# Transposing the later contexts on VectorE ahead of time, and shorter spreads, in a gated cross-attention kernel

## The chip, the cores and the metric

The kernel runs on one core of a Trainium2 chip. The metric is the device time of one launch in microseconds, a median over runs. Five engines take instructions in order, each from its own queue: TensorE (matmuls and transposes through an identity; PE in the profile, its weight loads PEld), VectorE (DVE), ScalarE (ACT), GpSimd (POOL) and SyncE (SP), which here issues nearly all DMAs. TensorE writes to PSUM, which has eight banks of 128 partitions by 512 floats; all else works in SBUF with 128 partitions. Semaphores let one engine wait for another.

## The reference

All data are float32. Four batches have 256 queries of width 512 and a context of 1601 rows of width 512. First comes cross-attention with 32 query heads of width 128 in 8 groups, each group with one key head and one value head; then a feed-forward step with eight low-rank experts.

```
q = (layernorm(x) @ Wq + bq).reshape(B, L, 8, 4, 128)
k, v = split(ctx @ Wkv + bkv)            # 8 heads of 128 each
attn = softmax(einsum('blkgd,bmkd->bkglm', q, k) / sqrt(128))
o = einsum('bkglm,bmkd->blkgd', attn, v)
x = x + tanh(g_xattn) * (o @ Wo + bo)
h = layernorm(x)
x = x + tanh(g_ffn) * (h @ base_W.T + 2 * sum over the top 2 of 8 experts)
```

## The kernel before

**Groups.** The main loop runs over 64 groups: batch b (4), key head h (8), half l of the queries (2). I number them 0 to 63 in that order, so batch 0 has groups 0 to 15. One group scores 128 queries of four heads (512 columns) against 1601 keys in 13 tiles, 12 of 128 rows and one of 65. `score_unit` (L1142) makes the scores for one or two tiles, ScalarE copies them out (L1151) and VectorE folds them into a running maximum (`fold`, L1067 to L1073). `softmax` spreads the maximum, subtracts it (L1181), takes the exponential (L1184), and folds a sum. `av_unit` (L1233) multiplies the group before with V: `run_group` alternates the scores of this group with the V products of the previous one. Then `window(now)` fills the time with other TensorE work, the tasks: key and value products of the next pair of heads (`pair_steps`, L896 and L907), query products, output products.

**Spread.** The maxima stand per partition and must go to all partitions (`spread`, L1076). VectorE joins two halves (L1106), transposes in 32x32 blocks (L1107), reduces each block (L1086) to 16 values per partition. Three copies bring the four groups of 32 partitions side by side (L1090), a second reduction joins them (L1093), three copies bring the result back to all four groups (L1097), and a transpose of the broadcast value spreads it (L1100). For the sums, the copies are made on GpSimd and the reciprocal stands between; for the maxima all is on VectorE.

**Block products.** The key, value and query products use Strassen's scheme with seven block products instead of eight. They need the context turned (features on partitions) and three sums of its four blocks, and one block replaced by a difference. A block is a half of the context rows by a half of the features. The turned context stands in `ctxT` (both halves of the rows, 801 columns each with the 65 rows left over split in two, and a column of zeros), the sums in `T`, the left-over rows in `rest`.

**Later contexts.** Batch 0's context is turned in the opening stretch. For batches 1 to 3 `ctx_steps` does it in one place: as soon as the last value pair of the batch before has used `ctxT` (group 12, 28 or 44), its 13 steps each load 128 context rows (L672), transpose four 128x128 blocks on TensorE into a bank (`turn_ctx`, L258), have ScalarE copy them to `ctxT` (L260), and after every second tile queue three subtractions on VectorE (`ctx_sums`, L723). `last_sums` (L734, L738) makes the last differences. After that the key products of the new batch's first pair can begin.

**Planner.** The order on each engine is written out by a planner that runs in Python while the program is built. It keeps a clock for TensorE (`now`), VectorE and ScalarE. `later` puts a piece of VectorE or ScalarE work with a cost and a ready time into one of ten queues (`sub`, `oT`, `so`, `exp`, `ln`, `T`, `norm`, `sum`, `low`, `low_a`). `pump` takes the piece that can start first, and of equals the one in the earlier queue. `force` takes a piece and all that it needs at once. A task has steps with a cost, a ready time and a due group. Weights are planned to be there 6000 ns after their load is issued (`LAG_PAIR`), context tiles 1700 ns (`LAG_CTX`). Buffers that exist once (`wq`, `wkv`, `wo`, `ctxT`, `T`) make a load wait on SP until the last reader is done. Weights and their sums are stored to DRAM when first made, in batch 0 for the most part, and loaded ready-made afterwards.

## Time and profile before

| what | value |
|---|---|
| median of 3 runs | 2557.84 us (2557.19 to 2559.42) |
| span of the profiled execution | 2555.5 us; the page gives no other time for it |
| TensorE busy | 2547.3 us |
| VectorE busy | 2202.6 us |
| ScalarE busy | 1188.1 us |
| GpSimd busy | 150.4 us |
| DMA | 167.16 MB, mean 65 GB/s |

Busy time is the union of an engine's instructions, without those that only wait or issue DMAs. Each float32 matmul appears as two records, each transpose as one. Matmuls are pipelined, so their records overlap: the cost of one is the distance to the next start, not its duration. The groups 13, 29 and 45, which hold the transposes of contexts 1 to 3, lie at 579.7 to 617.9, 1161.3 to 1192.5 and 1823.8 to 1861.2 us.

### The profile page before, as it was taken

The numbers are of one execution on the slowest core, as the hardware profiler recorded it, in microseconds if no ns is written. First come the engines' busy times: TensorE is split into PE (matmuls) and PEld (weight loads), VectorE is DVE, ScalarE is ACT, GpSimd is POOL, SyncE is SP. The second block draws the span as 40 slices with busy tenths as digits, with TensorE's granted clock in tenths as the row PEclk, the third lists the DMA queues.
The fourth block names the chain that finished last, engine by engine and source line by source line (L and its number), as shares of the span: only waits on it lengthen the run. The fifth ranks groups of instructions, "written<-read, shape, count | busy, mean of one in ns | idle before, by whom it ended". The sixth has DMA issues, their size and how long they took to land.

```text
span 2555.5 us, 26175 instructions
## 1 busy us (share of the span) xinstructions
PE 2547.3 (100%) x9235; PEld 1487.8 (58%) x9235; DVE 2202.6 (86%) x3310; ACT 1188.1 (46%) x1897; POOL 150.4 (6%) x401
## 2 busy tenths in 40 slices
PE   9999999999999999999999999999999999999999
PEld 7557566565555656455565665756656455555554
DVE  4889898899889989899788887878889899998897
ACT  3544454445434555455444444445454445544551
POOL 0000000000000000110000000000000000000000
PEclk9999999999999999999999999999999999999999
DMA  4313222324110111012121111212221011111000
GB/s 158 123 64 108 87 95 84 114 85 149 48 56 23 44 52 56 25 40 83 49 81 37 62 52 62 81 48 81 85 84 56 25 52 52 52 44 52 17 17 33
DMA packets 75499, 167.16 MB, mean 65 GB/s; under 512 B 5372, under 2 KB 32028, under 8 KB 72808
## 3 DMA queue, kind: packets, MB, share of 16 engines
q1 hardware_dynamic: 74424, 164.41, 19.3%
q8 instruction: 73, 1.20, 0.2%
q0 software_dynamic: 416, 0.81, 0.1%
q14 instruction: 58, 0.48, 0.1%
q10 hardware_dynamic: 528, 0.26, 0.0%
HBM read 119.06 MB, written 46.40 MB: 65 GB/s over the span
## 4 chain that ended last, share of the span: by engine, by line
PE 99%; DVE 1%; DMA 0%; ACT 0%; issue 0%; DVEq 0%; ACTq 0%
PE av L1233 28%; PE sc L1142 28%; PE pxk L896 6%; PE pxv L907 6%; PE pxq L896 4%; PE pyk L896 3%; PE pyv L907 3%; PE po L1310 3%; PE pox L484 3%; PE pyq L896 2%; PE pzk L896 2%; PE pzv L907 2%; PE poy L484 1%; PE pzq L896 1%; PE ptv L1020 1%; PE pk L803 1%
## 5 line engine op out<-in xcount | busy, mean ns | idle before, releaser
L1142 PE MATMUL sc<-qT,kT 128*128 128x512 f32 (+1 forms) x1664 | 775.9, 592 | 0.0
L1151 ACT COPY p<-sc 65x512 f32<-65x512 f32 x820 | 474.3, 586 | 636.5 <-PE sc L1142 575.2
L1233 PE MATMUL av<-p,v 65*128 65x512 f32 x1640 | 766.1, 592 | 1.2 <-ACT p L1184 1.2
L1233 PEld LDWEIGHTS av<-p,v 65*128 65x128 f32 x1640 | 309.5, 190 | 376.2 <-issue 370.8
L1142 PEld LDWEIGHTS sc<-qT,kT 128*128 128x128 f32 (+1 forms) x1664 | 307.0, 186 | 374.3 <-issue 340.4
L1181 DVE TENSOR_TENSOR p<-p,mb 65x512 f32<-65x512 f32 x442 | 485.9, 1137 | 0.1
L1184 ACT ACTIVATE p<-p 65x512 f32<-65x512 f32 x442 | 423.1, 990 | 38.6 <-DVE p L1181 34.5
L1073 DVE TENSOR_TENSOR mx<-mx,p 128x1024 f32<-128x1024 f32 x252 | 308.1, 1223 | 137.9 <-ACT p L1151 134.8
L1073 DVE TENSOR_TENSOR sm<-sm,p 128x1024 f32<-128x1024 f32 x252 | 307.4, 1220 | 9.8
L1090 POOL COPY quad_sm<-quad_sm 32x16 f32<-32x16 f32 x186 | 70.7, 380 | 2088.3 <-DVE quad_sm L1086 2083.1
L896 PE MATMUL pxq<-xq,wq 128*128 128x256 f32 x512 | 131.2, 379 | 0.0
L941 ACT ACTIVATE kT<-pxk,biasT 128x384 f32<-128x384 f32 (+1 forms) x120 | 57.9, 508 | 141.8 <-PE pxk L896 141.0
L896 PEld LDWEIGHTS pxq<-xq,wq 128*128 128x128 f32 x512 | 92.5, 189 | 31.2 <-issue 15.3
L941 ACT ACTIVATE qT<-pxq,biasT 128x256 f32<-128x256 f32 x64 | 30.3, 473 | 140.2 <-PE pxq L896 140.2
L944 ACT COPY v<-pxv 128x384 f32<-128x384 f32 x90 | 43.0, 477 | 104.8 <-PE pxv L907 104.8
L896 PE MATMUL pxk<-T,wk 128*128 128x417 f32 (+1 forms) x240 | 90.4, 499 | 0.0
L907 PE MATMUL pxv<-wv,T 128*128 128x128 f32 x720 | 90.2, 275 | 0.0
L896 PE MATMUL pxk<-ctxT,wk 128*128 128x417 f32 (+1 forms) x240 | 90.0, 499 | 0.0
L907 PE MATMUL pxv<-wv,ctxT 128*128 128x128 f32 x720 | 90.0, 275 | 0.0
L907 PEld LDWEIGHTS pxv<-wv,T 128*128 128x128 f32 x720 | 86.4, 192 | 4.7 <-issue 4.3
L907 PEld LDWEIGHTS pxv<-wv,ctxT 128*128 128x128 f32 x720 | 86.4, 192 | 4.7 <-issue 4.3
L1067 DVE TENSOR_TENSOR mx<-p,p 128x1024 f32<-128x1024 f32 x63 | 76.8, 1220 | 13.1 <-ACT p L1151 12.8
(264 smaller groups left out, 2809.6 us busy)
## 6 DMA issues: line engine op xcount, KB each, us to landing
wo<-in_L_xattn_Wo_dram SPq DMA_DIRECT2D x18, 1024.0 KB, 5.3
kept_q<-wq SPq DMA_DIRECT2D x16, 896.0 KB, 4.8
wq<-kept_q SPq DMA_DIRECT2D x16, 896.0 KB, 5.1
wo<-kept_wo SPq DMA_DIRECT2D x13, 1024.0 KB, 5.8
wk<-kept_k SPq DMA_DIRECT2D x11, 896.0 KB, 4.6
wv<-kept_v SPq DMA_DIRECT2D x11, 896.0 KB, 4.4
ctx<-in_ctx_dram SPq DMA_DIRECT2D x36, 256.0 KB, 2.7
wq<-in_L_xattn_Wq_dram SPq DMA_DIRECT2D x32, 256.0 KB, 3.1
```

The costliest lines, as they stand in the source:

```text
L484: nc.tensor.matmul(bk[:, :HD], left[i]()[:, c, :], blk[:, c, :], start=first and c == 0, stop=c == 1, skip_group_check=True,)
L896: nc.tensor.matmul(bk[:, :n], a(SLOT[i], c), operand(i, c, s, n), start=first and c == 0, stop=c == 1, skip_group_check=True,)
L907: nc.tensor.matmul(bk[:, t * HDIM : (t + 1) * HDIM], operand(i, c, s + t * P, P), a(SLOT[i], c), start=first and t == 0 and c == 0, stop=c ...
L941: nc.scalar.activation(dst, src, AF.Identity, bias=bias_of(kind, h0 + f))
L1067: nc.vector.tensor_tensor(acc, p[first], p[first + 1], op)
L1073: nc.vector.tensor_tensor(acc, acc, p[j], op)
L1142: nc.tensor.matmul(sc[:r, :], kT_t[b, h][:, key_col(i) : key_col(i) + r], qT_t[b, h][:, :, l * P : (l + 1) * P], start=True, stop=True,)
L1151: nc.scalar.copy(p[:r, k, :], sc[:r, :])
L1181: nc.vector.tensor_tensor(p, p, m, ALU.subtract)
L1184: nc.scalar.activation(p, p, AF.Exp, scale=scale)
L1233: nc.tensor.matmul(av, v_t[b, h][:r, i, :], p_t[key][j][:r, k, :], start=(j == 0 and k == 0), stop=(j == NPAIR - 1 and k == len(pairs[j]) ...
L1310: nc.tensor.matmul(po, oT_t[key][:, g, :], w_t["o", b, h][:, g, :], start=(g == 0), stop=(g == G - 1),)
```

## The change

**Later contexts.** `ctx_steps` no longer loads or transposes. A new function `swap_ctx(b, n)` handles one of 13 units of a context, early. A unit is 128 rows from each half of the context by half of the features (the 13th: 64 of the 65 left-over rows). Two SP loads bring the four pieces into one staging buffer of 128 by 512, VectorE transposes it in 32x32 blocks into a second buffer, three subtractions make four further planes, and eight stores (four for the 13th unit) write both buffers to a DRAM tensor `kept_ctx` of 2048 rows by 801 columns, in pieces of 32 floats. The DRAM addresses complete the transpose, since each block goes to its place. The very last context row goes a way of its own, with two small loads, three small subtractions and two small stores. The pieces go into a new, last queue `turn`.

Units of contexts 1 and 2 are called from group 0 on, one ahead of each group, a second one behind the scores of groups 1, 4, 7, 9 and 10, and none in groups 16, 17, 19, 21, 22 and 23; those of context 3 from group 32 on, one per group. A unit first forces the unit before it to be stored. `ctx_steps` then loads `ctxT`, `T` and `rest` with eleven SP loads from `kept_ctx`, when the last value pair of the batch before is done; `LAG_CTX` is 40000 ns. One subtraction on `rest` is left for VectorE. GpSimd clears the column of zeros for batch 0 only.

**Spread.** The three copies and the second reduction become two pairwise operations on VectorE, between the upper and lower 64 and then 32 partitions; the way back is two copies instead of three (32 to 64 partitions, then 64 to 128). For the sums only the way back is on GpSimd.

**x steps.** The layernorm steps and the first query weights of batch 2 become a task two groups earlier (ahead of group 21 instead of 23), due two groups earlier (28 instead of 30).

```diff
@@ -122,7 +122,7 @@
     clock = {"now": 0.0, "v": 0.0, "a": 0.0, "hold": 0.0}
     free = [0.0] * NBANK
     done = {}
-    queues = {q: deque() for q in ("sub", "oT", "so", "exp", "ln", "T", "norm", "sum", "low", "low_a")}
+    queues = {q: deque() for q in ("sub", "oT", "so", "exp", "ln", "T", "norm", "sum", "low", "low_a", "turn")}
 
     def vec(ns, ready=None):
 
@@ -151,7 +151,7 @@
         fn()
         clock[engine] = start + ns
         if key is not None:
-            done[key] = start + ns + SEM + (GP_COPIES if key[0] == "part" and key[2] < 4 else 0)
+            done[key] = start + ns + SEM + (GP_COPIES if key[0] == "part" and key[2] == 3 else 0)
 
     def pump(until=NEVER, most=None):
 
@@ -582,7 +582,7 @@
         xa_t[b] = pool.tile([P, NL, D], F32, tag=f"xa{b}", name=f"xa_{b}", bufs=1)
     STAGE = 2
 
-    LAG_DMA, LAG_CTX, LAG_X = 2500, 1700, 3000
+    LAG_DMA, LAG_CTX, LAG_X = 2500, 40000, 3000
 
 
     JOINT = 2
@@ -643,9 +643,6 @@
         return [(0, ready, begin)] + [f(*t) for t in tiles for f in (norm, turn)] + [(0, 0, sums)]
 
 
-    ctx_order = [i + k * (HK // P) for i in range(HK // P) for k in range(2)]
-    ctx_order += range(FULL, KT)
-
     def ctx_col(i):
 
         half, t = divmod(i, HK // P)
@@ -658,46 +655,113 @@
     def new_ctx(b):
         ctxT_t[b] = pool.tile([P, NC, 2 * HW], F32, tag="ctxT", name=f"ctxT_{b}", bufs=1)
         rest_t[b] = pool.tile([P, NC, REST], F32, tag="rest", name=f"rest_{b}", bufs=1)
-        if REST0 < HT:
+        if REST0 < HT and b == 0:
 
             nc.gpsimd.memset(ctxT_t[b][:, :, REST0:HT], 0.0)
 
+    ctx_kept = {}
+    NUNIT = HK // P * 2 + 1
+
+    def swap_ctx(b, n):
+
+        if n:
+            force(("kept", b, n - 1))
+        else:
+            ctx_kept[b] = dram.tile([8 * D // 2, HW], F32, tag=f"ctx_{b}", name=f"kept_ctx_{b}")
+        kept_b = ctx_kept[b].rearrange("(j k) w -> k j w", k=32)
+        m, q = divmod(n, 2)
+        src, dst = (
+            pool.tile([P, 4, P], F32, tag="stage", name=f"{kind}_{b}_{n}", bufs=STAGE)
+            for kind in ("ctx", "swap")
+        )
+        last_n = n == NUNIT - 1
+        r = 64 if last_n else P
+        for half in range(2):
+            if last_n:
+                assert REST == 65 and REST0 == 32
+                k0 = FULL * P + 32 * half
+                for c in range(2):
+                    nc.sync.dma_start(
+                        src[32 * c : 32 * c + 32, half::2, :],
+                        ctx_kv[b, k0 : k0 + 32, :].rearrange("k (s q c) -> k q s c", s=2, q=2)[:, c],
+                    )
+            else:
+                k0 = half * HK + m * P
+                nc.sync.dma_start(
+                    src[:, half::2, :],
+                    ctx_kv[b, k0 : k0 + P, :].rearrange("k (s q c) -> k q s c", s=2, q=2)[:, q],
+                )
+
+        flat = lambda t: t[:r].rearrange("k s c -> k (s c)")
+
+        def sums(S, R):
+            nc.vector.tensor_tensor(R[:, 0:2], S[:, 1::2], S[:, 0:2], ALU.subtract)
+            nc.vector.tensor_tensor(R[:, 2], S[:, 3], R[:, 0], ALU.subtract)
+            nc.vector.tensor_tensor(R[:, 3], S[:, 2], R[:, 2], ALU.subtract)
+
+        def swap():
+            nc.vector.transpose(flat(dst), flat(src))
+
+        def store():
+            for a in range(r // 32):
+                lo, q_ = (0, a) if last_n else (HT + m * P + 32 * a, q)
+                for i, t in enumerate((dst, src)):
+                    j = (2 * q_ + i) * 16
+                    nc.sync.dma_start(
+                        kept_b[:, j : j + 16, lo : lo + 32],
+                        t[32 * a : 32 * a + 32].rearrange("k s (j w) -> k (s j) w", w=32),
+                    )
+
+        later("turn", "v", 710, clock["now"] + LAG_DMA, swap)
+        later("turn", "v", 900, 0.0, lambda: sums(dst[:r], src[:r]), ("swap", b, n))
+        later("turn", "v", 0, ("swap", b, n), store, ("kept", b, n))
+        if last_n:
+            one = small.tile([P, 8, 2], F32, tag="one", name=f"one_{b}", bufs=1)
+            nc.gpsimd.memset(one, 0.0)
+            for i in range(2):
+                nc.sync.dma_start(
+                    one[:, 1 + 2 * i], ctx_kv[b, LK - 1, :].rearrange("(s q p) -> p s q", s=2, q=2)[:, i]
+                )
+
+            def end():
+                for q_ in range(2):
+                    nc.sync.dma_start(
+                        ctx_kept[b].rearrange("(q o p) w -> p q o w", q=2, o=8)[:, q_, :, HT - 1],
+                        one[:, :, q_],
+                    )
+
+            later("turn", "v", 500, clock["now"] + LAG_DMA, lambda: sums(one[:, :4], one[:, 4:]), ("swap", b, n + 1))
+            later("turn", "v", 0, ("swap", b, n + 1), end, ("kept", b, n + 1))
+
     def ctx_steps(b):
 
...
         def begin():
+            force(("kept", b, NUNIT))
             new_ctx(b)
             new_sums(b)
...
+            ct, rest, (T, tt) = ctxT_t[b], rest_t[b], T_t[b]
+            kept_b = ctx_kept[b].rearrange("(q o p) w -> p o q w", q=2, o=8)
+            for dst, o in (
+                (ct[:, 0:2, :HW], 0),
+                (ct[:, 2:4, :HW], 2),
+                (T[:, 1], 6),
+                (ct[:, 0:2, HW:], 5),
+                (T[:, 0], 4),
+                (T[:, 2], 7),
+                (ct[:, 2:4, HW:], 3),
+                (rest[:, 0:2, :REST0], 0),
+                (rest[:, 2:4, :REST0], 2),
+                (rest[:, 0:2, REST0:], 1),
+                (rest[:, 2:4, REST0:], 3),
+            ):
+                nc.sync.dma_start(dst, kept_b[:, o, :, : dst.shape[-1]])
+            later(
+                "T", "v", 250, clock["now"] + LAG_CTX,
+                lambda: nc.vector.tensor_tensor(tt, rest[:, 2:4], rest[:, 0:2], ALU.subtract),
+                ("T", "kv", b),
+            )
+
+        return [(0, ("pair", "v", b - 1, NKV // 2 - 1), begin)]
 
     def new_sums(b):
         t = pool.tile([P, 6 * HW + 2 * REST], F32, tag="T", name=f"T_{b}", bufs=1)
@@ -743,7 +807,7 @@
         if i < FULL:
             lo = ctx_col(i)
             transpose_rows(
-                src, P, ctxT_t[b][:, :, lo : lo + P], f"ctx_{b}_{i}", b > 0 or i % 2 == 1
+                src, P, ctxT_t[b][:, :, lo : lo + P], f"ctx_{b}_{i}", i % 2 == 1
             )
             return
 
@@ -823,7 +887,7 @@
     def first_k_steps(b):
 
         steps = sum(pair_steps("k", b, 0, lambda: next_weights("v", b, 0)), [])
-        return [(0, ("ctx", b), lambda: last_sums(b))] + steps
+        return steps
 
     def plain_v_steps(b, hp):
 
@@ -1079,34 +1143,30 @@
 
 
 
-        q = small.tile([P, 4, NB], F32, tag="quad", name=f"quad_{nm}", bufs=2)
         m = small.tile([P, NB], F32, tag="quadm", name=f"quadm_{nm}", bufs=2)
 
         def quadrants():
-            nc.vector.tensor_reduce(
-                q[:, 0, :], acc[:, 1, :].rearrange("p (c k) -> p c k", k=32), AX.X, op
-            )
-            for a in range(1, 4):
-                eng.tensor_copy(q[:32, a, :], q[32 * a : 32 * a + 32, 0, :])
+            nc.vector.tensor_reduce(m, acc[:, 1, :].rearrange("p (c k) -> p c k", k=32), AX.X, op)
+            nc.vector.tensor_tensor(m[:64], m[:64], m[64:], op)
+            nc.vector.tensor_tensor(m[:32], m[:32], m[32:64], op)
 
         def whole():
-            nc.vector.tensor_reduce(m[:32], q[:32].rearrange("p a c -> p c a"), AX.X, op)
             if after is not None:
                 after(m[:32])
-            for a in range(1, 4):
-                eng.tensor_copy(m[32 * a : 32 * a + 32], m[:32])
+            for r in (32, 64):
+                eng.tensor_copy(m[r : 2 * r], m[:r])
 
         def back():
             nc.vector.transpose(
                 res.rearrange("p (c k) -> p c k", k=32), m.unsqueeze(2).to_broadcast([P, NB, 32])
             )
 
-        own = 550 if eng is nc.vector else 0
+        own = 340 if eng is nc.vector else 0
         return [
             (690, lambda: nc.vector.tensor_tensor(acc[:, 0, :], acc[:, 0, :], acc[:, 1, :], op)),
             (710, lambda: nc.vector.transpose(acc[:, 1, :], acc[:, 0, :])),
-            (690 + own, quadrants),
-            (250 + own + (270 if after is not None else 0), whole),
+            (690 + 340, quadrants),
+            (own + (270 if after is not None else 0), whole),
             (710, back),
         ]
 
@@ -1867,7 +1927,11 @@
     tasks.append(Task(steps, 0))
 
     prev = None
+    swaps = deque()
+    TWICE, IDLE = (1, 4, 7, 9, 10), (16, 17, 19, 21, 22, 23)
     for hi, (b, h) in enumerate(heads):
+        if h == 0:
+            swaps.extend((c, n) for c in {0: (1, 2), 2: (3,)}.get(b, ()) for n in range(NUNIT))
         pair, coming = (b, h // 2), next_pair(b, h // 2)
         nxt = heads[hi + 1] if hi + 1 < len(heads) else None
         for l in range(NL):
@@ -1875,10 +1939,14 @@
             cur = (b, h, l)
             if cur == last:
                 break
-            if (h, l) == (NKV - 5, 1) and b + 1 < B and (b + 1) % JOINT == 0:
+            if (h, l) == (NKV - 6, 1) and b + 1 < B and (b + 1) % JOINT == 0:
                 load_pair("q", b + 1, 0)
                 tasks.append(Task(x_steps(b + 1), now + 7))
+            if swaps and now not in IDLE:
+                swap_ctx(*swaps.popleft())
             run_group(cur, prev)
+            if swaps and now in TWICE:
+                swap_ctx(*swaps.popleft())
             if prev is not None:
                 steps = out_steps(prev)
                 if steps:
```

More of the change, by code (lines that the diff above doesn't have):

```diff
@@ L660, in new_ctx @@
         rest_t[b] = pool.tile([P, NC, REST], F32, tag="rest", name=f"rest_{b}", bufs=1)
-        if REST0 < HT:
+        if REST0 < HT and b == 0:
             nc.gpsimd.memset(ctxT_t[b][:, :, REST0:HT], 0.0)
-    def ctx_steps(b):
-        staged = {}
-        def load(n):
-            i = ctx_order[n]
-            s = pool.tile([P, D], F32, tag="stage", name=f"ctx_{b}_{i}", bufs=STAGE)
-            nc.sync.dma_start(s[: rows[i]], ctx_kv[b, i * P : i * P + rows[i], :])
-            staged[i] = s
+    ctx_kept = {}
@@ L675, in begin @@
+    def ctx_steps(b):
         def begin():
+            force(("kept", b, NUNIT))
             new_ctx(b)
             new_sums(b)
-        def step(n):
-            def run():
-                i = ctx_order[n]
-                if n + STAGE - 1 < KT:
-                    load(n + STAGE - 1)
-                turn_ctx(b, i, staged.pop(i))
-                if n % 2 == 1 and i < FULL:
-                    ctx_sums(b, ctx_col(i) - HW, P)
-                if i == FULL:
-                    ctx_sums(b, 0, HT)
-                if n == KT - 1:
-                    done["ctx", b] = clock["now"] + 1000
-            return NC * TR_COST, LAG_CTX, run, True
@@ L693, in first @@
-        def first():
-            for n in range(STAGE - 1):
-                load(n)
-        return [(0, 0, first), (0, ("pair", "v", b - 1, NKV // 2 - 1), begin)] + [
-            step(n) for n in range(KT)
-        ]
+            ct, rest, (T, tt) = ctxT_t[b], rest_t[b], T_t[b]
[14 more added lines that the diff above has]
+                nc.sync.dma_start(dst, kept_b[:, o, :, : dst.shape[-1]])
```

## The prediction

> **What bounds the kernel now.** I read the page's busy shares first, then the chain that ended last. Times are microseconds unless marked ns.
>
> ```profile
> PE 2547.3 (100%) x9235; PEld 1487.8 (58%) x9235; DVE 2202.6 (86%) x3310; ACT 1188.1 (46%) x1897; POOL 150.4 (6%) x401
> PE 99%; DVE 1%; DMA 0%; ACT 0%; issue 0%; DVEq 0%; ACTq 0%
> ```
>
> TensorE is busy 2547.3 of 2555.5, and 99% of the chain lies on it. Busy time alone could hide gaps, so I read the order of time of group 29 (1161.3 to 1192.5), the thinnest of the three stretches that hold the removed context transposes.
>
> ```profile
> 1166.87 0.60 PE L258 MATMUL pt_ctx<-ident,ctx 128*128 128x128 f32 x4
> 1167.31 1.88 PE L1233 MATMUL av<-p,v 128*128 128x512 f32 x4
> ...
> 1192.30 0.41 PE L258 MATMUL pt_ctx<-ident,ctx 65*128 65x65 f32 x4
> 1192.55 2.74 PE L1142 MATMUL sc<-qT,kT 128*65 128x512 f32 x6
> 1196.49 1.13 PE L1233 MATMUL av<-p,v 65*128 65x512 f32 x2 [1.20 <-ACT p L1184]
> ```
>
> The distance from one start to the next is what an instruction costs: four transposes of a full tile 0.44 (1166.87 to 1167.31), the 65-row tile 0.25 (1192.30 to 1192.55). Matmuls stand shoulder to shoulder; the one gap is 1.20, where the first product with V waits for an exponential. So whatever leaves TensorE leaves the time, as long as its feeders keep up. The next busiest is VectorE, by batch (first four rows) and in four single groups. Columns: stretch, length, busy time of PE, weight loads, DVE, ACT, POOL, then granted clock, DMA share, GB/s.
>
> ```profile
> 61.40:697.70 636.30, 636.30 (x2328) 381.81 (x2327) 567.99 (x880) 303.00 (x486) 35.94 (x92) 1.00 0.28 95
> 697.70:1293.70 596.00, 594.80 (x2131) 334.23 (x2129) 533.19 (x768) 287.71 (x453) 46.73 (x97) 1.00 0.15 50
> 1293.70:1940.10 646.40, 646.40 (x2402) 391.30 (x2401) 530.66 (x791) 295.86 (x478) 30.70 (x98) 1.00 0.21 66
> 1940.10:2555.50 615.40, 610.95 (x2088) 331.88 (x2087) 540.78 (x814) 283.92 (x439) 33.22 (x94) 1.00 0.12 40
> ...
> 414.90:458.60 43.70, 43.70 (x133) 24.55 (x132) 38.92 (x64) 19.14 (x31) 1.48 (x6) 1.00 0.23 77
> 458.60:497.30 38.70, 38.70 (x117) 21.68 (x116) 34.72 (x54) 17.60 (x28) 1.13 (x6) 1.00 0.31 106
> ...
> 1124.30:1161.30 37.00, 37.00 (x163) 22.37 (x162) 35.65 (x49) 16.88 (x27) 8.73 (x13) 1.00 0.15 49
> 1192.50:1249.40 56.90, 55.70 (x168) 29.90 (x167) 53.36 (x75) 28.50 (x46) 2.69 (x6) 1.00 0.19 60
> ```
>
> VectorE is at 89% in batch 0 and 82% in batch 2, where the new work is put. It has run at 96% for a group (1124.3, 35.65 of 37.0) with TensorE never idle, and at 94% (1192.5) with 1.2 idle. That is the tolerance I measure the addition against. Prices come from these groups:
>
> ```profile
> L1107 DVE STREAM_TRANSPOSE mx<-mx 128x512 f32<-128x512 f32 x64 | 45.5, 711 | 2.2
> L1090 DVE COPY quad_mx<-quad_mx 32x16 f32<-32x16 f32 x192 | 31.5, 164 | 3.9
> L723 DVE TENSOR_TENSOR T<-ctxT,T 128x256 f32<-128x256 f32 x36 | 15.3, 425 | 1.1
> L723 DVE TENSOR_TENSOR T<-ctxT,T 128x66 f32<-128x66 f32 x6 | 1.4, 225 | 0.1
> ```
>
> **The change part by part.** The sum is made against the profiled span, 2555.5; the page gives no other time of that execution, and the median of the runs, 2557.84, stands 2.3 above the span. I carry that 2.3 unchanged.
>
> Removed from TensorE: per context 12 full tiles at 0.436 (the mean over five in group 29) and one short at 0.25, so 5.48, times three contexts: **-16.4**. All of it lies on the path. Their ACT evictions (39, at 0.59 and 0.38) go too, worth nothing while ACT is at 46%; POOL's three clears and 39 SP loads go as well.
>
> Removed wait: the 1.20 of group 29. There three subtractions of the old context work (1.35) ran between the last maximum and the spread. Without them, and with a spread of 3.5 instead of 4.3, the exponential is ready some 7 after the last score (fold 0.9 + 1.2, spread 3.5, subtraction 0.7, exponential 0.6), and TensorE has 9.4 of work until it needs it (two V units 3.43, output 3.43, next scores 2.57). The transposes were cover there and 2.4 is left, so **-1.2**. Late next is nothing nearer than this 2.4; with group 13's query products, 6.0 more cover it.
>
> Added on VectorE: 39 units of one 128x512 transpose (0.711), one 128x256 subtraction (0.42) and two of 128x128 (0.285 each, between the rows for 66 and 256 columns): 1.70 per unit, 66.3 in all, plus 9 tiny ones of about 0.2 for the last context row. Removed there: per context 18 subtractions at 0.42, three at 0.22, and the two wide last sums (1.02 + 0.95), 10.2; three times 30.6. Spread of a maximum: six copies at 0.165 and a reduction of 0.25 become two copies and two 16-column operations; the latter lie between 0.164 (copy) and 0.241 (reciprocal of the same 32x16), I take 0.19. Saving 0.53 x 64 = 34. Spread of a sum: the 0.24 reduction becomes two such operations, +0.14 x 62 = 9; three of six 0.38 POOL copies in a row fall out ahead of it and the other three become two. Net on VectorE about +12 of 2203. By batch it is uneven: batch 0 gets 21 units (36) less 16 x 0.53 (8.5) less 10.2, so 568 + 17 in 636 - 5.5: 93%. Leaving out the old context work, groups 1 to 12 rise by 1.2 each, and the five that hold two units by 2.9: 458.6 goes from 34.7 to 37.6 of 38.7, 97%; 414.9 from 38.9 to 41.8 of 43.7, 96%. Batch 1 gets five units and loses 18.7, batch 2 gets 13 at 82%. Five groups near 97% at 0 (the 96% row) to 1.2 (the 94% row) of TensorE idle: 0 to 6, I take **+2.5**. If the cover (idle VectorE) is gone, it is the first rival.
>
> Added on SP and the DMA rings: per unit two loads of 256 rows of 512 B and eight stores of 512 rows of 128 B (64 KB), ten issues at about 0.33 of SP time. Each store waits on SP for VectorE's sums, and behind it queue the weight loads. The packet records show 27 ns per 512-B row and 84 ns per 2-KB row; no data row under 512 B is stored in this trace. A store gives each of 16 engines 32 rows: at 11 ns (five 128-byte instruction fetches) 0.35, at 84 ns 2.7; I take the nearest data row, 27 ns, 0.86, so 7 per unit and 270 per engine over the run, about a tenth of the DMA's time. Kept weights land 22 to 30 before their use, which covers it. First-time weights do not: their VectorE sums follow the landing by 0.7 to 4 in batch 0, 22 such loads. Five double groups, each with one load late by one store, beyond a slack of about 2: 0 to 3, I take **+1**. VectorE's transpose in turn waits for its load: the planner counts 2.5 from the issue, the rows show 2.7 to 3.1 to landing and the second load is issued 0.33 later, so up to 1 per unit; behind it stand the folds and subtractions of the running group, and TensorE waits for those. It is planned behind everything else that is ready, mostly well after the load, so I take 0 and leave the rest to rival A.
>
> Here a rule speaks against the change. The Trainium skill, "DMA: Bandwidth & Descriptors", Specifications, asks for at least 512 B per row for full rate and says that below it the engine reads, modifies and writes. By that rule, if it means two passes, a row would cost 54 ns, a unit 14, and the term would be about 2 instead of 1; no run shown here has such a row.
>
> Context loads: 6.56 MB per context in eleven DMAs in place of transposes. The 1-MB row below lands in 5.8, so serially 36; by 7-KB rows (272 ns each on 16 engines) about 16. The loads start at the end of groups 12, 28 and 44 (1158.0 for context 2); the first key products in group 30 come after its 22 of scores, some 51 later, and the planner's own due time is 40. **0.** Other transfers (queries, output weights) queue behind it, but the latter have 25 or more of slack.
>
> ```profile
> wo<-kept_wo SPq DMA_DIRECT2D x13, 1024.0 KB, 5.8
> wq<-in_L_xattn_Wq_dram SPq DMA_DIRECT2D x32, 256.0 KB, 3.1
> ctx<-in_ctx_dram SPq DMA_DIRECT2D x36, 256.0 KB, 2.7
> ```
>
> The next batch's x steps begin two groups earlier. Their SP load of query weights (896 KB, lands in 5.1) goes past two groups' loads of other weights into a buffer idle since group 15; the x loads on SP, the bias load on POOL and the rest still wait for the same output of the batch's third head. **0**, or below 1 with the cover gone: one load late by 5.1 against 22 or more of slack. Sum: 2557.8 - 16.4 - 1.2 + 2.5 + 1 = **2543.7**.
>
> A second rule: the skill's "VectorE: DVE Perf Modes", Rules for kernel authors, says two SBUF inputs should start in the same quadrant of 32 partitions, and the new pairwise maxima break it. By it such an instruction starts only after all earlier ones end, which these do anyway, each needing the one before; the sum would stay.
>
> **The rivals.** (A) VectorE fills up in batch 0 and passes its delay on. For it: 97% in the double groups, and units that are not done by the next unit are forced in ahead of subtractions. Against: 96% without a gap. Price: 36 + 5 x 0.14 - 8.5, about 28 if all is exposed: 2540.2 + 28 = 2568. It ends slower once more than 63% (17.6) of it shows; less gives 2545 to 2557. (B) The short stores hold up first-time weights. At the 84-ns end a unit takes 21.5 of each ring; with one late weight of 3 in each of five double groups 2540.2 + 15 = 2555. (C) The context load is late: beyond 51 after its start, each further microsecond comes three times; at 55, 2544 + 12 = 2556. Against: 16 to 36. (D) No stall at all: 2540.2. That the change doesn't do its work can't be for the transposes, which are gone from the program.
>
> **How the numbers follow.** A run of this kernel tells about 0.2% (5.1) from no change: the runs span 2557.19 to 2559.42. Chances: forecast, with D as its lower edge, 2540 to 2548: 0.68; A 0.18 (slower in 0.08 of it, same 0.03); B 0.09 (slower 0.03, same 0.02); C 0.05 (slower 0.03, same 0.01). So faster 0.80, same 0.06, slower 0.14. Range: below D's 2540 lies little; up to 2555 leaves out the bad halves of A, B and C.
>
> **What will show it.** Right: no context transposes after 45 us, TensorE's busy share still near 100%, the wait of V's product at the start of group 30 gone, batch 0's VectorE near 93%. Wrong: V products waiting for exponentials, or score copies for sums, in groups 1 to 12 (A); VectorE waiting for DMAs of wq, wk, wv or of the staged contexts (B); key products of a new context waiting for DMA (C).

## The result, and where the time went

The changed kernel takes 2617.88 us (median; 2615.94 to 2619.50) against 2557.80 for the kernel before: a ratio of 1.0234, 95% interval 1.0223 to 1.0245. The prediction, 2543.7 and faster, has the wrong sign. Times below are microseconds unless marked ns.

First the busy shares and the chain that ended last, from the page of the kernel after.

```profile
PE 2550.8 (98%) x9079; PEld 1479.5 (57%) x9079; DVE 2206.0 (84%) x3276; ACT 1164.5 (45%) x1854; POOL 74.7 (3%) x153
PE 89%; DVE 5%; DMA 4%; SPq 1%; issue 1%; ACT 0%; DVEq 0%; ACTq 0%
```

TensorE did less, yet its busy time rose by 3.5: part of its work ran at a lower clock, of which more below. VectorE rose by 3.4 in busy time and fell in share. What is new is the chain: 9% of it (235 us) lies on VectorE and DMAs, where there was 1%. To take the clock out I counted TensorE's work by start-to-start prices (a matmul record of N columns counts N/1.2 ns plus 2, so 0.43 for 512 columns and 0.11 for 128, a fit to the starts in the groups without a gap): 2528.7 before, 2512.4 after. What remains of the span is 26.8 before and 103.7 after. So the transposes did leave (-16.3), and 76.9 of something else came.

By batch, and in single groups of batch 0, from the table of stretches (length, then busy time of PE, weight loads, DVE, ACT, POOL, then granted clock, DMA share, GB/s):

```profile
61.50:734.30 672.80, 616.28 (x2132) 364.31 (x2131) 546.54 (x858) 276.52 (x446) 17.12 (x28) 0.95 0.54 113
734.30:1358.80 624.50, 624.45 (x2222) 349.97 (x2221) 560.65 (x788) 298.70 (x464) 19.53 (x37) 1.00 0.25 62
1358.80:1999.70 640.90, 640.90 (x2351) 385.60 (x2349) 536.67 (x794) 290.44 (x465) 17.54 (x33) 1.00 0.37 87
...
350.20:401.20 51.00, 44.20 (x182) 29.55 (x181) 39.70 (x64) 19.67 (x30) 0.00 (x0) 0.90 0.57 90
401.20:455.80 54.60, 43.91 (x190) 28.38 (x188) 35.66 (x52) 18.45 (x31) 0.38 (x2) 0.87 0.50 110
...
1259.10:1314.50 55.40, 55.40 (x166) 29.94 (x165) 49.31 (x65) 28.01 (x43) 0.38 (x2) 1.00 0.18 57
```

Batch 0 (first row) holds the loss: 56 without TensorE work and a clock of 0.95. Batches 1 and 2 have none, though they also handle units, at most one per group. In batch 0 TensorE waits for copies of scores, for VectorE's steps on the output products and for a copy of a value product (first four lines of its list of waits: total, times, longest):

```profile
PE sc L1202 <- ACT p L1211: 29.1, 6, 10.7
PE pox L484 <- DVE xa L462: 13.3, 3, 8.6
PE poy L484 <- DVE xa L490: 6.8, 1, 6.8
PE pyv L971 <- ACT v L1008: 6.0, 1, 6.0
```

Groups 7 and 8 (fourth and fifth row) have 40.9 of TensorE work each and last 51.0 and 54.6. In the same stretches VectorE is busy only 78% and 65%: it isn't full, it stands. What it stands for is the second line of its list of waits; the list of SP's waits gives the next link (total, times, longest).

```profile
DVE swap L703 <- DMA ctx<-in_ctx_dram: 77.0, 11, 15.0
```

```profile
SPq L690 <- DMA kept_ctx<-swap: 91.7, 17, 9.3
```

L703 is the 32x32 transpose of a unit; it waits for the load of the unit, eleven times, 77.0 in all, about the whole loss. L690 is the issue of that load; it waits for the *stores* of the unit before to land, since both use the same two staging buffers. Of the 77.0, 18.5 (four waits) falls on the second unit of a double group and 58.5 (seven waits) on a unit called ahead of a group, which forces the unit before it to be stored and loads at once. In order of time at the start of group 8, VectorE:

```profile
399.82 0.42 DVE L698 TENSOR_TENSOR ctx<-swap 128x256 f32<-128x256 f32 x1
400.27 0.29 DVE L699 TENSOR_TENSOR ctx<-swap,ctx 128x128 f32<-128x128 f32 x1
400.60 0.29 DVE L700 TENSOR_TENSOR ctx<-swap,ctx 128x128 f32<-128x128 f32 x1
...
401.92 0.24 DVE L1269 RECIPROCAL quadm_sm<-quadm_sm 32x16 f32<-32x16 f32 x1
417.18 0.71 DVE L703 STREAM_TRANSPOSE swap<-ctx 128x512 f32<-128x512 f32 x1 [15.02 <-DMA ctx<-in_ctx_dram]
417.81 1.18 DVE L1131 TENSOR_TENSOR sm<-p,p 128x1024 f32<-128x1024 f32 x1
```

and SP, which issues the DMAs:

```profile
400.92 1.66 SPq L710 DMA_DIRECT2D kept_ctx<-ctx  x3
402.61 1.20 SPq L710 DMA_DIRECT2D kept_ctx<-swap  x1
403.85 1.74 SPq L710 DMA_DIRECT2D kept_ctx<-ctx  x1
405.64 0.49 SPq L337 DMA_DIRECT2D kept_q<-wq  x1
413.79 1.20 SPq L690 DMA_DIRECT2D ctx<-in_ctx_dram  x2
```

One unit's last sum ends at 400.9 (L700). Its last stores are issued from 400.92 and land, by the trace, at 407.91, 409.98, 411.96, 413.73 and 414.59. The next unit's load starts at 413.79, just behind the 413.73. VectorE has had that unit's transpose at the head of its queue since 402.16 and starts it at 417.18. Behind it stand the folds; ScalarE waits 14.59 for them with its next score copy, and TensorE stops:

```profile
408.03 1.02 PE L1202 MATMUL sc<-qT,kT 128*128 128x512 f32 x2
419.74 2.07 PE L1202 MATMUL sc<-qT,kT 128*128 128x512 f32 x2 [10.69 <-ACT p L1211]
```

The DMA issues tell why the landing takes so long (KB each, median us from issue to landing).

```profile
kept_ctx<-swap SPq DMA_DIRECT2D x150, 64.0 KB, 5.6
kept_ctx<-ctx SPq DMA_DIRECT2D x150, 64.0 KB, 6.5
ctx<-in_ctx_dram SPq DMA_DIRECT2D x72, 128.0 KB, 6.2
```

A store of 64 KB in rows of 128 bytes lands after 5.6 or 6.5 (medians), the first of a burst after 3.7, and inside a burst each lands 1.57 (median) after the one before. Each of the 16 DMA engines has 32 of its rows, so a row takes 49 ns (1.57 / 32). The loads of the units, planned at 2.5, take 6.2 behind them. So the late stores act twice: by the times of issue in the trace, VectorE stood 27.5 of the 77.0 before the second load of the unit was even issued, and 49.5 from then to its landing.

Last, the clock. In two stretches around that stall (the DMA share of 1.19 counts packets that overlap):

```profile
401.20:412.00 10.80, 7.85 (x20) 3.14 (x17) 0.86 (x4) 2.23 (x4) 0.38 (x2) 0.96 1.19 155
412.00:422.00 10.00, 2.26 (x3) 1.17 (x4) 4.75 (x6) 1.71 (x4) 0.00 (x0) 0.50 0.47 103
```

TensorE's granted clock halves (0.50) in the stall and stays there for some time after it. The clock record has seven such stretches from 247 to 626, 61.4 together, and TensorE was busy for 33.9 of them; so at most 17 of the 76.9 is work at half speed, a consequence of the stalls and not their cause.

### The profile page after: what moved, and what is told of

Read it like the earlier page. It is cut to its first block, busy times and chain, and to the rows that moved or that the text cites. A ratio compares the mean times of both kernels' runs of the same rounds, so it can differ in the third digit from the quotient of the medians.

```text
span 2616.1 us, 26066 instructions
## 1 busy us (share of the span) xinstructions
PE 2550.8 (98%) x9079; PEld 1479.5 (57%) x9079; DVE 2206.0 (84%) x3276; ACT 1164.5 (45%) x1854; POOL 74.7 (3%) x153
## 4 chain that ended last, share of the span: by engine, by line
PE 89%; DVE 5%; DMA 4%; SPq 1%; issue 1%; ACT 0%; DVEq 0%; ACTq 0%
PE av L1293 25%; PE sc L1202 25%; PE pxk L960 6%; PE pxv L971 6%; PE pxq L960 4%; PE po L1370 3%; PE pyv L971 3%; PE pyk L960 3%; PE pox L484 3%; DMA ctx<-in_ctx_dram 2%; PE pyq L960 2%; PE pzk L960 1%; DMA kept_ctx<-swap 1%; PE pzv L971 1%; PE poy L484 1%; PE ptv L1084 1%
## 5 line engine op out<-in xcount | busy, mean ns | idle before, releaser
L1157 POOL COPY quadm_sm<-quadm_sm 32x16 f32<-32x16 f32 x124 | 66.4, 535 | 2411.0 <-DVE quadm_sm L1269 2407.1
L703 DVE STREAM_TRANSPOSE swap<-ctx 128x512 f32<-128x512 f32 (+1 forms) x39 | 27.3, 701 | 77.4 <-DMA ctx<-in_ctx_dram 77.0
```

The lines of the kernel that those rows point to most:

```text
L1157: eng.tensor_copy(m[r : 2 * r], m[:r])
```

## The experiments

Three causes were on the table. **S**: the way units are staged (two units in one group, two buffers, a transpose that VectorE has in its queue before its load can start). **A**: VectorE's own added work. **B**: the short rows of the stores. "Rest" below is the span less TensorE's work by the start-to-start prices: 26.8 before, 103.7 after. The kernel before took 2557.55 to 2557.99 beside these runs.

**One unit per group.** Edit against the changed kernel:

```diff
-    TWICE, IDLE = (1, 4, 7, 9, 10), (16, 17, 19, 21, 22, 23)
+    TWICE, IDLE = (), ()
```

> The changed kernel with one unit ahead of each group, never a second one, and no group left out (units 0 to 25 in groups 0 to 25). Theory S (staging): in the changed kernel a group with two units forces the stores of the first, the load of the second has to wait until these stores have landed because both use the same two staging buffers, and VectorE, already put in front of that load by the planner, stands still. Then without second units the 77 us of VectorE waits for staged contexts fall below 10 and the time is 2541 to 2546. Theory A (VectorE is full in batch 0): batch 0 still gets 16 units in place of 21, so some three quarters of the loss of 76 us stay: about 2590 to 2600. Theory B (rows of 128 bytes clog the rings): the same three quarters, 2590 to 2600.

Measured: 2565.07 (2562.26 to 2567.51), ratio 1.0027 (1.0015 to 1.0038); rest 50.8. The same units, transposes, sums and stores, spread over groups 0 to 25, cost 52.8 less, which is more than A and B allowed. The waits of the transpose in the kernel with one unit per group (a fourth, of 5.6, the list puts down to another load, but the unit's own landed 0.2 ahead of the transpose and the other after its start):

```profile
DVE swap L703 <- DMA ctx<-in_ctx_dram: 17.0, 3, 7.5
```

Most of S holds, but the time doesn't reach the forecast. The rest comes in groups 2, 8, 9 and 14 (6.3, 4.8, 7.5 and 3.0 over their work). In group 8 VectorE waits 5.9 for a first-time output weight, the victim that the prediction's rival B had named. In group 9 it has the same form as before: the sums of one unit are only done when the next one forces them (428.4 to 429.5), its last stores are issued from 429.50, the next load at 432.02 behind them, and VectorE waits 7.13 at 440.39. So one unit per group takes away the second load in a group, not the order "finish late, load at once".

**Twice the work.** On top of that edit, each unit is transposed and summed twice over, into the same places:

```diff
-            nc.vector.transpose(flat(dst), flat(src))
+            for _ in range(2):
+                nc.vector.transpose(flat(dst), flat(src))
...
-        later("turn", "v", 900, 0.0, lambda: sums(dst[:r], src[:r]), ("swap", b, n))
+        later("turn", "v", 2000, 0.0, lambda: [sums(dst[:r], src[:r]) for _ in range(2)], ("swap", b, n))
```

(The planner's cost of the transpose is doubled too.)

> As the run with one unit per group, but each unit transposes twice and makes its three subtractions twice, so VectorE gets 32 units' worth of work in batch 0 against 21 in the changed kernel; the data, loads and stores are the same. Theory S: the extra 1.7 us per group fit into VectorE's idle time, 2541 to 2552. Theory A: more work than in the changed kernel, so at least its time, 2615 or more. Theory B: the same as with one unit per group.

Measured: 2593.34 (2593.16 to 2594.09), ratio 1.0138 (1.0124 to 1.0152); rest 79.2. VectorE's busy time rose by 66.2 against the kernel with one unit per group, 44 of it in groups 0 to 25 (26 units of 1.70), where the loss lies; the time rose by 28.3. No transpose waits for a staged load now. Instead groups 7, 11, 20, 23 and 27 are 7 to 10 longer than their work, and ScalarE's score copies wait for VectorE's folds, 118.1 against 41.8 with the units done once:

```profile
ACT p L1212 <- DVE sm L1138: 118.1, 47, 5.0
```

So the expectation of S fails here, and so do those of A (2615 or more) and B (unchanged). VectorE's spare time in batches 0 and 1 is nearly used up by the units themselves, and more of the same shows at 0.64 of its price; that is a net figure, since the waits for staged loads (17.0 and 5.6) went at the same time. The loads themselves still wait on SP for stores, 206.4 in 46 times: a late load costs VectorE nothing as long as other work stands ahead of the transpose. A is not what slowed the changed kernel, where VectorE stood idle in the bad groups, but it is near.

**Long rows.** The changed kernel with its own schedule, but the stores write each 64 KB as 32 rows of 2 KB to one place. The context is then in the wrong order in DRAM: this kernel leaves out the part of the transpose that the addresses do.

```diff
-                    j = (2 * q_ + i) * 16
+                    at = (n * 8 + a * 2 + i) * 32 * 512
+                    long = ctx_kept[b].rearrange("r w -> (r w)")
                     nc.sync.dma_start(
-                        kept_b[:, j : j + 16, lo : lo + 32],
-                        t[32 * a : 32 * a + 32].rearrange("k s (j w) -> k (s j) w", w=32),
+                        long[at : at + 32 * 512].rearrange("(k f) -> k f", f=512),
+                        t[32 * a : 32 * a + 32].rearrange("k s c -> k (s c)"),
                     )
...
```

(The last unit of a context gets one store more, of 8 KB.)

> The changed kernel with its schedule, but each store writes rows of 2 KB to one place in DRAM, as many bytes as before, in place of rows of 128 bytes to their places; this leaves out the ordering of the context, so later batches compute on mixed-up contexts at the same cost. Theory S: the stores land in about 3 us in place of 6.4, so each wait of a load for them gets 3 to 4 us shorter, and of eleven VectorE waits of 3 to 15 us a good half is left: 2570 to 2600. Theory B: the loss goes, 2541 to 2550. Theory A: nothing changes, 2610 to 2620.

Measured: 2560.99 (2557.68 to 2563.84), ratio 1.0009 (1.0000 to 1.0019); rest 48.2. The same unit loads and stores, their order and VectorE's work cost 56.9 less. With long rows, the stores and loads land so (first two rows), and these are the waits of the transpose (last row, from the list of VectorE's waits):

```profile
kept_ctx<-swap SPq DMA_DIRECT2D x150, 64.0 KB, 1.7
...
ctx<-in_ctx_dram SPq DMA_DIRECT2D x72, 128.0 KB, 2.7
```

```profile
DVE swap L703 <- DMA ctx<-in_ctx_dram: 25.9, 6, 5.9
```

This lies below what S gave and above what B gave: two units in a group still leave six waits, but two thirds of the 77.0 went with the landing of the short rows. The edit changes the length of the rows and their addresses (one place in DRAM, not many) together; stores of 512-byte rows to many places come in the run with short rows on the loads, below, and land in 3.1 to 3.3 for 256 KB, so scattered addresses alone are not what costs.

**Both: one unit per group and long rows** (the two edits together; the ordering of the context is left out again).

> One unit per group with stores of 2-KB rows to one place in place of 128-byte rows; this leaves out the ordering of the context, at the same number of bytes and DMAs. Theory S: stores land in 1.7 us, VectorE's waits for staged contexts go, 2542 to 2550. Theory A: 2560 to 2567, as with short rows.

Measured: 2545.94 (2544.57 to 2546.42), ratio 0.9953 (0.9940 to 0.9967); rest 32.0, and the transposes' waits are down to 6.4. Either edit takes away 53 to 57, both together 71.9: they break the same chain in two places. What is left is 2.2 from the forecast. So the forecast's other terms were about right in sum; its +2.5 for double groups isn't tested here, as no group holds two units. Against the run with one unit per group (2565.07) only the stores differ, so a cause that lies in VectorE's work or its order alone would have left this kernel at 2560 to 2567.

**The spread alone.** The kernel before, with only the new spread (the two pairwise operations and the two copies back):

```diff
-            for a in range(1, 4):
-                eng.tensor_copy(q[:32, a, :], q[32 * a : 32 * a + 32, 0, :])
...
+            nc.vector.tensor_tensor(m[:64], m[:64], m[64:], op)
+            nc.vector.tensor_tensor(m[:32], m[:32], m[32:64], op)
...
-            for a in range(1, 4):
-                eng.tensor_copy(m[32 * a : 32 * a + 32], m[:32])
+            for r in (32, 64):
+                eng.tensor_copy(m[r : 2 * r], m[:r])
```

> The kernel before with the new spread alone (two pairwise operations and two copies). All theories: VectorE's busy time falls by about 25 us (34 for the maxima, less 9 for the sums), TensorE has almost no idle to give back, so 2556 to 2558; the 1.2 us wait at the start of group 30 may get shorter by up to 0.7.

Measured: 2560.86 (2559.91 to 2561.58), ratio 1.0011 (1.0002 to 1.0020); rest 30.4. VectorE's busy time falls by 24.0 (2202.6 to 2178.6), and the kernel gets 3 slower, not faster: groups 7, 13 and 62 now last 0.8 to 1.6 longer than their work (in 13 a context transpose waits 1.2 for its load, in 62 a product with V waits 1.2 for an exponential). The wait at the start of group 30 stays as it was, 1.20.

**Stored in its own group.** One unit per group, and each unit is finished behind the scores of the group in which it began, not when the next unit forces it:

```diff
-            if swaps and now not in IDLE:
-                swap_ctx(*swaps.popleft())
+            unit = swaps.popleft() if swaps and now not in IDLE else None
+            if unit:
+                swap_ctx(*unit)
             run_group(cur, prev)
-            if swaps and now in TWICE:
-                swap_ctx(*swaps.popleft())
+            if unit:
+                force(("kept", *unit))
```

> As the run with one unit per group, but each unit's transpose, sums and stores are forced right behind the scores of its own group instead of ahead of the next unit's load. VectorE's work, rows and bytes are the same; the stores now have the whole task phase (10 to 18 us) to land before the next load. Theory S (the next load waits for stores that land late, VectorE waits for that load): the 17 us of VectorE waits for staged contexts go and the time falls to 2542 to 2549. Theory A (VectorE's added work itself is what TensorE waits for; twice the work cost 28 us for 44 us more): nothing falls, 2562 to 2568.

Measured: 2552.75 (2548.78 to 2555.04), ratio 0.9979 (0.9970 to 0.9987); rest 38.9. With the short rows kept, this order is faster than the kernel before, though it lies between the two cases. Its waits for stores on SP and for staged loads on VectorE:

```profile
SPq L690 <- DMA kept_ctx<-swap: 86.0, 20, 8.1
DVE swap L703 <- DMA ctx<-in_ctx_dram: 5.9, 1, 5.9
```

The loads wait for the stores on SP nearly as long as in the changed kernel (91.7), but stores and load now land before VectorE's queue comes to the transpose; a single transpose still waits, 5.9 in group 14. Of the 12 that remain over the rest of the kernel before, 3.5 lie in that group and 6.8 in group 27, where VectorE is late with its folds.

**The same with the old spread** (`spread` as in the kernel before, all else as in the last one).

> The same as the run that stores each unit in its own group, with the old spread (three copies, reduction, three copies). VectorE has some 25 us more work over the run. Theory S: within 3 us of that run, perhaps below it, since the new spread alone cost 2.9 us. Theory A: 0.6 of the 11 us that fall on groups 0 to 27, so 5 to 8 us slower.

Measured: 2555.81 (2552.69 to 2558.73), ratio 0.9993 (0.9984 to 1.0002). Here the new spread is worth 3.1, where alone it cost 3. With the old spread VectorE waits 18.8 for first-time query weights (6 times; 3.6 with the new one), rival B's victim once more.

**Short rows on the loads.** As the kernel stored in its own group, but the loads fetch each 32x32 block to where its transpose belongs (16 loads of 16 KB in rows of 128 bytes per unit), so that after VectorE's transpose whole rows of 128 floats leave, in two stores of 256 KB with rows of 512 bytes. The planner counts 10 from the issue to the transpose. Core of the edit:

```diff
-                nc.sync.dma_start(
-                    src[:, half::2, :],
-                    ctx_kv[b, k0 : k0 + P, :].rearrange("k (s q c) -> k q s c", s=2, q=2)[:, q],
-                )
...
+                    k0 = half * HK + m * P
+                    f0 = s_ * 256 + q * P + 32 * g
+                    frm = ctx_kv[b, k0 : k0 + P, f0 : f0 + 32].rearrange("(c r) i -> r c i", r=32)
+                nc.sync.dma_start(to, frm)
...
-                    nc.sync.dma_start(
-                        kept_b[:, j : j + 16, lo : lo + 32],
-                        t[32 * a : 32 * a + 32].rearrange("k s (j w) -> k (s j) w", w=32),
-                    )
+                    nc.sync.dma_start(kept_b[q_][:, 4 * i : 4 * i + 4, lo : lo + w], t_)
```

> The run that stores each unit in its own group, with the short rows moved from the stores to the loads: a unit's source is laid out so that each 32x32 block stands where its transpose belongs, 16 loads of 128 rows of 128 bytes, and after the transpose two stores of 512 rows of 512 bytes. The result is complete. Theory S (stores with 128-byte rows land late and hold up the loads and weights behind them): stores land in 2 to 3 us, nothing is behind the loads that VectorE needs soon, and the time is that of long rows, 2544 to 2549. If short rows cost as much on the way in, the loads hold the rings as long as the stores did, and it stays at 2551 to 2556. Theory A: 2551 to 2555.

Measured: 2550.18 (2548.11 to 2551.16), ratio 0.9970 (0.9957 to 0.9982); rest 35.3. Its DMA issues:

```profile
ctx<-in_ctx_dram SPq DMA_DIRECT2D x576, 16.0 KB, 1.8
kept_ctx<-swap SPq DMA_DIRECT2D x36, 256.0 KB, 3.1
kept_ctx<-ctx SPq DMA_DIRECT2D x36, 256.0 KB, 3.3
```

The time lies between the cases. The records of 128-byte rows take 13 ns on the mean here, 95% of them at most 13, where the changed kernel's take 23 and 5% of them 73 or more. The same transpose of the same data, with its short rows on the way in, is complete and faster than both kernels. Against the kernel stored in its own group that is 2.6, of which the planner's 10 may have a part; no run takes the two apart. The sixteen loads cost SP more: they are issued 0.47 apart, and a unit's take 8.9 from the first issue to the last landing (medians).

**Short rows on the loads, finished only when the next unit forces it** (the same transfers, with the order of the kernel with one unit per group).

> The same loads and stores with a unit forced only ahead of the next unit's load, as in the run with one unit per group (2565). Theory S: the load of a unit has no late store in front of it, 2545 to 2552. Theory A: 2562 to 2568.

Measured: 2561.56 (2559.83 to 2564.50), ratio 1.0015 (1.0006 to 1.0024); rest 50.4. The time is near the case of A, but not for its reason: of the 23.6 that the rest is above that of the kernel before, 21.7 is one stall in group 13, which lasts 54.3 for 32.6 of work:

```profile
616.05 0.71 DVE L699 STREAM_TRANSPOSE swap<-ctx 128x512 f32<-128x512 f32 x1 [21.18 <-DMA ctx<-in_ctx_dram]
```

A unit's first two loads were issued at 587.5 and 588.0; the other fourteen only from 600.4 to 614.2, behind the loads of the next context (eleven, 5.88 MB), with VectorE waiting since 594.9. It is the mechanism of the changed kernel with another transfer in front.

**The same as the short loads, with batch 2's x steps two groups later**, as in the kernel before:

```diff
-            if (h, l) == (NKV - 6, 1) and b + 1 < B and (b + 1) % JOINT == 0:
+            if (h, l) == (NKV - 5, 1) and b + 1 < B and (b + 1) % JOINT == 0:
```

> The kernel with the short rows on the loads (2550.18), with the x steps of batch 2 put back to two groups later, as in the kernel before. If its stall of 6.7 in group 27 comes from those steps' place, it goes: about 2543.5 to 2546 (the 1.2 wait of V's product at the start of group 30 may come back in part). If it comes from VectorE's load in that part of batch 1, it moves to a neighbouring group: 2549 to 2553.

Measured: 2549.18 (2548.73 to 2551.30), ratio 0.9969 (0.9956 to 0.9981); rest 34.9. The time lies where the second case put it, but the stall didn't move: group 27 is as long as before (45.1 for 38.3 of work). The place of the x steps is worth nothing that can be told, and it isn't the cause of that stall. VectorE is 91% busy in that group and doesn't stand for long; why just this group falls behind is open.

**The same as the short loads, with the old spread.**

> The kernel with the short rows on the loads (2550.18), with the old spread. If the new spread is worth its saving on VectorE wherever VectorE is loaded, as in the pair with short stores (2552.75 against 2555.81): about 2553. If what it does is a matter of where the planner's order happens to leave a wait, as alone on the kernel before (+2.9), anything from 2546 to 2553, with single stalls in other groups.

Measured: 2557.14 (2554.71 to 2558.33), ratio 0.9997 (0.9988 to 1.0006); rest 42.6. That is above both cases. The new spread is worth 7 here, 3.1 in the other pair and -3 alone. It saves VectorE the same 24 each time; with units on VectorE there is use for that, and what is beyond that probably comes from where the planner's order leaves its small waits (5.0 in group 7, 3.9 in 13, 7.5 in 23 here); no run shows why there.

**Planned later.** The changed kernel, with the planner told 10 instead of 2.5 from a unit's loads to its transpose:

```diff
-        later("turn", "v", 710, clock["now"] + LAG_DMA, swap)
+        later("turn", "v", 710, clock["now"] + 10000.0, swap)
```

> The changed kernel (2617.88), in which the planner counts 10 instead of 2.5 from the issue of a unit's loads to its transpose. If VectorE stands still because the transpose is put in front of a load that the planner believes to be there: the waits of the transposes for staged loads (77.0) fall well below half, where one unit follows another in the same group they stay, since a unit that is forced is put in at once; the time 2570 to 2600. If the waits come from the stores alone and no place of the transpose helps (each unit is forced anyway): 2610 to 2625.

Measured: 2607.61 (2604.49 to 2609.29), ratio 1.0194 (1.0180 to 1.0208); rest 93.9. The time lies between the two cases. The waits for staged loads go down to 38.7 and one of 6.9 that the list puts down to a store, but other things wait now:

```profile
DVE swap L703 <- DMA ctx<-in_ctx_dram: 38.7, 8, 12.3
DVE xa L436 <- DMA wo<-in_L_xattn_Wo_dram: 10.7, 2, 5.6
DVE wq L351 <- DMA wq<-in_L_xattn_Wq_dram: 9.2, 3, 6.3
```

```profile
SPq L690 <- DMA kept_ctx<-swap: 148.6, 33, 8.4
```

The load of nearly every unit now waits on SP for the stores of the one before (33 times for 148.6, where it was 17 for 91.7), and the first-time weights issued behind it come late: the 10.7 and 9.2 were 0 and 1.4. A truer number in the planner is worth 10 of the 60, so its delay alone isn't the cause.

## Why the prediction was wrong, point by point

**TensorE, -16.4.** Right: 16.3.

**The wait in group 29's order, -1.2.** Group 30 of the kernel after is 55.40 long with TensorE busy for 55.40 (last row of the stretches above), so the wait is gone there. The new spread isn't what removed it: alone it left the wait at 1.20. One of the same kind and size, a product with V waiting for an exponential, now stands in group 62, as it does with the spread alone. Net nothing.

**VectorE, +12 net, +2.5 on the path.** The amounts were right, if anything high: +3.4 measured; the transpose takes 0.701, the pairwise operations 0.170 and 0.164 where I took 0.19. Nothing shows that the pairwise operations across partition groups of 32 cost more. In the changed kernel VectorE wasn't the bound; the run with twice the units' work shows that it then becomes so.

**SP and the DMA rings, +1.** Here a size was wrong, and the step below made it matter. I took 27 ns per 128-byte row from the 512-byte loads, as the nearest data row, so 0.86 per store and 7 per unit. Measured: 49 ns, 1.57 per store in a burst, 12.6 per unit, and 5.6 to 6.5 from issue to landing (medians), where 2-KB rows land in 1.7. That is inside the bounds I gave (11 to 84 ns). The rule that I weighed, that below 512 B per transfer the engine reads, modifies and writes (the Trainium skill, "DMA: Bandwidth & Descriptors", Specifications; I read it per row), would have made it 54 ns by my own estimate of two passes; the runs come near that on the way out (49), and stay well below it on the way in (at most 23, see the last section).

**"VectorE's transpose in turn waits for its load ... so I take 0."** This is the step that failed: the term that I put at 0 came to 77.0 of standing on VectorE. I looked for those who would wait for a late store among the first-time weights, a few microseconds each. But the first who waits is the next unit: it has the same two buffers, so its load cannot be issued until the stores have landed, and the planner puts its transpose into VectorE's queue at the load's issue plus 2.5. I left out the wait ahead of the load's issue (27.5 of the 77.0), and counted its landing at 2.7 to 3.1, as if no store were in front of it on the rings (49.5). From the last sum of one unit to the transpose of the next took 16.3 in group 8 (400.9 to 417.2), and 15.0 of it VectorE stood with the folds behind it. I had written that it is "planned behind everything else that is ready"; but `pump` takes the piece that can start first and goes by the order of the queues only among equals, so 2.5 after the issue the transpose stands ahead of folds that become ready later, and a unit that is forced is put in at once. No run has more than two staging buffers; whether these would do without the other edits is open.

**The context loads, 0, and the x steps, 0.** Both right, though what is loaded per context is 5.88 MB (seven loads of 801 KB and four of 32 or 33 KB), not 6.56, which is the size of the whole `kept_ctx`. The first groups after the context loads (14, 30) are as long as their work, though the loads land 9.3 to 10.8 after their issue; moving the x steps back changes nothing.

**The rivals.** B had the right source and, for this kernel, the wrong victim: 2555 at its worst, since it counted five late weights and no wait for staged contexts, though that wait stands among its signs. First-time weights cost VectorE 1.9 here; they do wait in other orders (6.3 and 0.8 with one unit per group, 18.8 and 1.5 stored in its own group with the old spread, 21.3 planned later). One of A's signs, score copies waiting for sums in batch 0, did appear, but with VectorE at 65 to 81% in the groups that stall; no product with V waits for an exponential there. C did not come up: no key product of a new context waits for a DMA. The range stopped at 2555 because the one step whose wait I had set to 0 was given no upper end of its own; the 77.0 that it came to would have put it near 2620.

## What to carry to other kernels

Price a transfer with short rows by its landing, per row and per engine, and then ask first who reuses its buffer and what is issued behind it: where load, work and store share one pair of buffers, the whole chain (last sum, store, landing, load, landing) must fit into the time between two units, or the instruction at its end must not stand in an engine's queue ahead of other work. Finishing each unit in its own group did the latter here: SP still waited 86.0 for the stores, VectorE only 5.9 for the loads. If a transpose by addresses needs short rows on one side, put them on the loads: here that was worth 2.6 and 3.5 in the two pairs of runs (with a truer number in the planner besides). Finishing each unit in its own group alone turned +2.3% into -0.2%, both together into -0.3%. And read an engine's share in the bad stretch itself: a share that falls while the time grows says that the engine waits, not that it is full.

## What the runs showed of the hardware that was not expected

Rows of 128 bytes cost 49 ns per engine when stored to DRAM (1.57 per 64 KB in a burst; 1.46 to 1.53 with one unit per group, stored in its own group and planned later). Loaded from DRAM they cost at most 23: where the 16-KB loads, 8 rows per engine, queue behind one another, each lands 0.18 (median) after the one before. The stored rows go to DRAM rows of 3204 bytes and the loaded ones come from rows of 2048; no run separates that from the direction. The records of the kernel with the short stores have a median of 13 ns and a mean of 23, so most of the 49 doesn't show in them; only landing times tell it.

After stalls of some microseconds TensorE's granted clock is 0.5 in stretches of 3.4 to 13.7, in the run with late short loads 20.5. In the changed kernel each of the seven gaps of 3.7 to 10.7 in TensorE's work in batch 0 goes with such a stretch, and one of 2.6 doesn't. All stretches that lie wholly within a run are multiples of 3.413, which fits a window of that length as described in the Trainium skill, "TensorE: Matmul & The Clock Gate", Part 1. So a stall costs more than its length, here up to 17 on top of some 60.

A load of 256 KB in sixteen pieces, issued around 5.88 MB of other loads from the same engine, kept VectorE waiting for 21.2; a piece lands in 1.8 (median), and the sixteen of a unit take 8.9 from the first issue to the last landing.
